# A graph layer on one core: the edge lists' test for order leaves the head, three of four lists go to the edge loop, and the order between stages changes

## The chip, the core and the metric

The kernel runs on one NeuronCore of a Trainium2 chip, as one program from its first load to its last store. The core has four engines that compute, each with an instruction queue of its own that runs in order: TensorE (PE in the profile, its weight loads PEld), VectorE (DVE), ScalarE (ACT) and GpSimd (POOL). A fifth, SyncE (SP), only issues transfers (DMA). Engines wait for each other and for transfers by semaphores. [...]

The metric is the time of one execution on the device in microseconds (us); less is better. Before the change three runs gave a median of 3995.82 us (3989.85 to 4008.74). The profiled execution took 4023.54 us.

## The reference

One layer of a graph network over 6250 nodes with 256 features, 200000 edges that come sorted by their destination, and a second list of 131072 edges in no order. Cut to what matters:

```python
def gat(h, W, a_src, a_dst, src, dst):            # 4 heads of 64
    z = einsum('ni,hid->nhd', h, W)
    es, ed = einsum('nhd,hd->nh', z, a_src), einsum('nhd,hd->nh', z, a_dst)
    e = leaky(es[src] + ed[dst], 0.01)
    ex = exp(e - segment_max(e, dst)[dst])
    alpha = ex / segment_sum(ex, dst)[dst]
    return segment_sum(alpha[:, :, None] * z[src], dst)

def reference(x, src, dst, ...):
    xn = layernorm(x)
    x = x + gat(xn, W, a_src, a_dst, src, dst) + mix(xn, Wqkv, Wout, gamma)
    return x + ffn(layernorm(x), W_gat, ..., W1, b1, W2, b2, edge_index)
```

`mix` is linear attention with 8 heads (softmax of q over features and of k over nodes, then two small matmuls, Wout and a layer norm with `gamma`). `ffn` lets four experts work on each node. How much each counts comes from a second attention over the unordered edges, with 16 features a node, whose sums are normalised with `ln_gamma` and `ln_beta`; the best two experts of a node are mixed.

The input of the first list is sorted, but the kernel has to be right for any list.

## The kernel before

**Tiles.** Nodes are cut into NT = 49 tiles of 128 (the last has 106). Edges are cut into chunks of 128. A chunk's 128 source rows are gathered by one indirect DMA from a table in DRAM, one row for each partition, and summed over destinations by a matmul with a one-hot matrix. For the sorted list every tile gets K1 = 33 chunks, the last 28, so S1 = 1612 chunks in all. Two lists, `src_c` (row to gather) and `dl_c` (which of the tile's 128 nodes), hold what each chunk needs; a copy of the second, `rows_1`, goes to DRAM, to be read back broadcast over the partitions.

**The head** (0 to 138 us) makes the table `ztab` and the lists, side by side:

- `load_x` (L507) loads XB = 7 tiles of x. `project_x` (L520) takes seven tiles at a time: statistics (L527, L528), their rstd chain (L132 to L136, one for the seven), the normalised tile `xn` (L533), two transposes into `ln_tp` (L146), the copy to `xy` (L537), the matmuls into `zp` (L540), the copies into one of eight `zt` buffers (L542 on ACT, L545 on DVE), and the store of the table's rows (L547, on SP's queue).
- Meanwhile `bd` and `bs` (destinations and sources of all edges, 13 blocks of 128 by 128) and `nx` (the destinations moved by one) are loaded on the same queue. `down` (L598) compares `bd` with `nx`: any edge whose destination exceeds the next one's shows an unordered list. The maximum of it (L600) becomes `flag` (L605), which all engines read into a register. Under `tc.If(unordered != 0)` (L610) stands `order_edges`, which sorts the list. Both lists are then stored to DRAM as `d_ord` and `s_ord` (L617), ordered in any case.
- Borders (L629 to L669): the destinations are cast to `fd` (L630), compared with all tile borders (`lt`, L640), counted by matmuls (`cp`, `row`), which gives `start_k`, the edge at which each tile begins. From it, with matmuls into `ip` (L682), comes `at` (L689): where in the ordered list each chunk begins.
- POOL gathers the chunks' edges with 26 indirect DMAs (L697), 13 for each list.
- `lists(b0)` (L705 to L721) is called for b0 = 0, 4, 8 and 12, each call for four blocks of 128 chunks (the last for one). It corrects and masks the local destinations (L708, L712, L713), stores `rows_1` (L714), and transposes both lists through the PSUM tile `e_tp` (L720) into `src_c` and `dl_c` (L721).
- `over` (L742) is set when a tile has more edges than its chunks hold.
- Weights of `mix` are loaded on SP's queue (L753 to L755) behind the table store of tile 41.
- With all of the table stored, the largest source term is found (L198, L190) and the edge loop's gathers begin.

**The edge loop** (138 to 2638 us) takes 202 groups of eight chunks. `FirstEdges` holds a group: gathers (L784), the attention weights, the weighing of gathered rows (`weigh`, L848), the one-hot matrices (`one_hot`, L813), and the matmuls into the tile's sums `ag` (L857). The body for one group, with the parts of the next group between its own, is

```python
            now.weigh(0, 4)
            nxt.terms()
            now.add(sums, g * G1, 0, 4)
            now.weigh(4, 8)
            nxt.one_hot()
            now.add(sums, g * G1, 4, 8)
            groups[g + 2].one_hot_t()
            nxt.terms_sum()
            nxt.sources()
```

with steps of `mix` and sorting steps for the second edge list in the gaps. A finished tile is divided by its weights' sum (L766 to L768), added up (L866), normalised (`n_st` L158, `n_mv` L159, L168), multiplied by `W_gat`, and stored in the second table (`htab` and `htab_0`, L181 and L182).

**Branch and second stage** (2638 to 4022 us). Under `tc.If(many != 0)` (L1116), with `many` read from `over`, stands a slow general path that redoes the first attention for lists which do not fit. With the inputs here it is skipped. The second stage takes the unordered edges in 98 groups (`SecondEdges`, gathers L1321), with the experts' matmuls (L1427, L1447) between. In its group 2 the rows `ln_gamma` and `ln_beta` are loaded and multiplied by a quarter (L1778), and a mask `first_of` is set (L1779 to L1781).

**What sets the order.** A scheduler orders each engine's instructions when the kernel is built, from what each one depends on; the order in the source is not binding. `tc.issue_after(i)` keeps what stands under it behind instruction i. DMA transfers started by SP pass through SP's queue in order, as do the indirect ones through POOL's.

Of the kernel before, what the change touches and what calls it, by code (L numbers as in the profile page):

```python
# [9 lines left out]
F32 = mybir.dt.float32  # L10
# [10 lines left out]
P = 128  # L21
# [43 lines left out]
def gps_layer(ctx: ExitStack, tc: tile.TileContext, a: dict, out: bass.AP):  # L65
# [83 lines left out]
    def second_norm(work, ps, ts_):  # L149
# [15 lines left out]
        for i, t in enumerate(ts_):  # L165
# [15 lines left out]
            SP.dma_start(htab_0[n0 : n0 + n, :], h_all[:n, t, 0:HF])  # L181
            SP.dma_start(htab[n0 : n0 + n, 0:HW], h_all[:n, t, 0:HW])  # L182
# [80 lines left out]
    rows_1 = dram.tile([BS * P * P, 1], BF16, name="rows_1")  # L263

    def order_edges(w, bs, bd):
# [81 lines left out]
        V.tensor_copy(bd, both[:, :, :, 1])  # L347

# [150 lines left out]
    with tc.tile_pool(name="a_x", bufs=1) as ax, tc.tile_pool(name="a_w", bufs=3) as aw, tc.tile_pool(  # L499
# [69 lines left out]
        with tc.tile_pool(name="e_w", bufs=1) as w:  # L569
            bs = w.tile([P, B1, P], I32, name="bs")  # L570
# [3 lines left out]
            G.memset(bs[:, last:], 0)  # L574
            G.memset(bd[:, last:], NT * P)
            G.memset(nx[:, (E1 - 1) // (P * P) :], int(FAR))
            load_blocks(bd, a["dst"], E1)
            load_blocks(nx, a["dst"][1:E1], E1 - 1)
            load_x(XB)
            load_blocks(bs, a["src"], E1)  # L580
# [15 lines left out]

            down = w.tile([P, B1, P], BF16, name="down")
            V.tensor_tensor(down, bd, nx, op=OP.is_gt)  # L598
            d1 = w.tile([P, 1], F32, name="d1")
            V.tensor_reduce(d1, down.rearrange("p b j -> p (b j)"), AX.X, OP.max)  # L600
            flag = w.tile([1, 1], I32, name="flag")
            with tc.tile_pool(name="fl_p", bufs=1, space=PSUM) as ps:
                d2 = ps.tile([1, 1], F32, name="d2")
                T.matmul(d2, d1, ones[:, 0:1], start=True, stop=True)
                V.tensor_scalar(flag, d2, 1.0, None, op0=OP.min)  # L605
            project_x(XB)
            unordered = nc.values_load(
                flag[0:1, 0:1], min_val=0, max_val=1, skip_runtime_bounds_check_because="a count of 0s and 1s, at most 1"
            )
            with tc.If(unordered != 0):  # L610
                with tc.tile_pool(name="ord_w", bufs=1) as ow:
                    order_edges(ow, bs, bd)

            load_x(3 * XB)
            project_x(2 * XB)
            for ord_, b_ in ((d_ord, bd), (s_ord, bs)):
                SP.dma_start(ord_.rearrange("(b r j) o -> r b (j o)", r=P, j=P), b_)  # L617
            with tc.tile_pool(name="e_l", bufs=1) as w, tc.tile_pool(name="e_p", bufs=1, space=PSUM) as ps:
                NX = NT - 1
                room = kx.rearrange("p t d -> p (t d)")  # L620
                used = 0

                def take(a_, b_, dt):
                    nonlocal used
                    used += a_ * b_
# [1235 lines left out]
```

## Time and profile before

| | |
|---|---|
| median of three runs | 3995.82 us (3989.85 to 4008.74) |
| profiled execution | 4023.54 us, its span 4021.7 us |
| mean granted clock of TensorE | 0.784 |
| head | 0 to 138 us |
| edge loop, 202 groups | 138 to 2638 us |
| second stage, 98 groups | 2638 to 4022 us |
| first and last list gather (POOL, L697) | start at 63.79, the last one ends near 96 us |
| first table gather (POOL, L784) | 138.12 us |
| last table gather of the loop (L784) | 2613.98 us |
| first gather of the second table (L1321) | 2642.17 us |

The profile's page gives busy times for the whole span; a stage has to be cut out by its limits in time. In a row of the time line the columns are start, duration, engine, line and operation, tiles written and read with their shapes, how many instructions the row joins, and in brackets how long the engine had been idle before it and what ended that. A suffix q (DVEq, PEq) means the engine's instruction sequencer rather than its arithmetic. "remote" and "issue" stand for a release that the profile does not trace to an instruction.

The page's slices show the span in 40 equal parts, each digit the busy share in tenths:

```profile
PE   5666677755564555546555555446666767677766
DVE  5566666677774776766677566625555546565657
POOL 2466666665665666656666566655556556555552
PEclk8778798877776777777777777767888788888878
```

### The profile page before, as it was taken

Reading aid. Unit: us, or ns where it says so; the run is one execution under the profiler, and the core shown is the slowest. Engines: PE = TensorE matmul, PEld = TensorE weight load, DVE = VectorE, ACT = ScalarE, POOL = GpSimd, SP = SyncE. Lnnn points to the kernel's source line nnn. Section 1 sums busy time; section 2 is a strip of 40 time slices with the busy share of each in tenths; the row PEclk is TensorE's granted clock in tenths of the full one; section 3 lists DMA queues with packets and bytes.
Section 4 is the critical chain, followed back from the end, with each engine's and each line's share of the span. In section 5 each row is a group of like instructions: output and inputs, shape, how many; then the busy total and the mean of one; then the engine's idle time right before and its main releaser. Section 6 shows DMA issues by size and latency. Waiting matters only on the chain. (4 is left out here: it accounts for less than half of the span.)

```text
span 4021.7 us, 36890 instructions
## 1 busy us (share of the span) xinstructions
PE 2498.4 (62%) x10919; PEld 1773.3 (44%) x10920; DVE 2464.6 (61%) x6571; ACT 506.5 (13%) x1319; POOL 2328.2 (58%) x2436
## 2 busy tenths in 40 slices
PE   5666677755564555546555555446666767677766
PEld 4444565544443444434444433324444444444444
DVE  5566666677774776766677566625555546565657
ACT  2200011111110110111111111121111011111112
POOL 2466666665665666656666566655556556555552
PEclk8778798877776777777777777767888788888878
DMA  5443344444443443444444444332222123222221
GB/s 166 131 114 109 108 116 110 119 119 116 122 130 97 116 123 108 120 112 115 133 116 127 113 125 109 104 81 51 45 60 50 42 49 81 53 61 57 59 56 32
DMA packets 248565, 388.33 MB, mean 97 GB/s; under 512 B 73447, under 2 KB 156279, under 8 KB 248090
## 3 DMA queue, kind: packets, MB, share of 16 engines
q0 software_dynamic: 103296, 230.96, 23.1%
q1 hardware_dynamic: 142893, 154.04, 12.6%
q8 instruction: 91, 1.49, 0.1%
q14 instruction: 129, 1.05, 0.1%
q10 hardware_dynamic: 2156, 0.80, 0.1%
HBM read 345.44 MB, written 40.15 MB: 96 GB/s over the span
## 5 line engine op out<-in xcount | busy, mean ns | idle before, releaser
L784 POOL DMA_INDIRECT gt<-ztab,src_c x1612 | 1551.5, 962 | 967.3 <-issue 406.3
L857 PE MATMUL ag<-gt,oh 128*128 128x260 f32 x3224 | 1017.2, 474 | 342.6 <-DVE gt L848 232.0
L1321 POOL DMA_INDIRECT gt<-htab,src x784 | 748.6, 955 | 595.3 <-DVE dv L1390 261.2
L857 PEld LDWEIGHTS ag<-gt,oh 128*128 128x128 f32 x3224 | 754.0, 241 | 527.2 <-DVE gt L848 255.0
L1427 PE MATMUL hp<-xy,w 128*128 128x512 f32 (+1 forms) x832 | 444.3, 657 | 187.2 <-ACT hT L1432 140.5
L1447 PE MATMUL yo<-w,hT 128*128 128x256 f32 x1568 | 446.4, 425 | 111.4 <-issue 63.8
L848 DVE TENSOR_TENSOR gt<-gt,dv 128x1040 f32<-128x1040 f32 x403 | 489.0, 1224 | 13.7 <-issue 12.6
L1447 PEld LDWEIGHTS yo<-w,hT 128*128 128x128 f32 x1568 | 316.5, 209 | 246.2 <-issue 137.2
L883 PE MATMUL m<-wqkv,xy 128*128 128x256 f32 (+1 forms) x784 | 254.6, 464 | 169.5 <-DVE kmax L894 85.3
L1427 PEld LDWEIGHTS hp<-xy,w 128*128 128x128 f32 x832 | 169.0, 216 | 328.5 <-issue 167.3
L883 PEld LDWEIGHTS m<-wqkv,xy 128*128 128x128 f32 (+1 forms) x784 | 171.8, 231 | 217.2 <-DVE kmax L894 91.3
L813 DVE TENSOR_TENSOR oh<-dv,dl_c 128x1024 f32<-128x1024 f32 x202 | 244.0, 1208 | 7.8 <-PE ag L857 5.2
L1432 ACT ACTIVATE hT<-hp,b 128x512 f32<-128x512 f32 (+1 forms) x208 | 133.5, 660 | 479.4 <-remote 172.9
L1371 DVE TENSOR_TENSOR e_sel<-ed,ohq 128x384 f32<-128x384 f32 x98 | 54.1, 552 | 182.4 <-remote 136.8
L213 ACT ACTIVATE src_f<-src_d,shift_c 128x32 f32<-128x32 f32 x202 | 64.9, 321 | 772.5 <-DVE src_d L798 441.4
L381 DVE MAX8 src<-dl 128x8 f32<-128x1024 f32 x128 | 155.5, 1215 | 0.0
L383 DVE MATCH_REPLACE8 dl<-src,dl 128x1024 f32<-128x1024 f32 x127 | 153.5, 1209 | 0.0
L976 PE MATMUL m<-m_sb,qT 128*128 128x256 f32 (+1 forms) x196 | 74.4, 516 | 125.4 <-ACT qT L973 86.8
L1412 DVE TENSOR_REDUCE ag<-ag 128x40 f32<-128x120 f32 x98 | 27.2, 277 | 193.5 <-remote 154.5
L828 PE MATMUL ed<-pw,ohT 128*128 128x24 bf16 x1612 | 71.8, 176 | 106.7 <-DVE ohT L822 46.3
L828 PEld LDWEIGHTS <-ohT 128*128 128x128 bf16 x1612 | 67.1, 100 | 141.6 <-DVE ohT L822 53.6
L836 DVE TENSOR_REDUCE pw<-ed 128x64 f32<-128x192 f32 x202 | 69.6, 344 | 94.9 <-remote 74.6
(374 smaller groups left out, 2745.7 us busy)
## 6 DMA issues: line engine op xcount, KB each, us to landing
br<-rows SPq DMA_DIRECT2D x299, 256.0 KB
gt<-ztab,src_c POOLq DMA_INDIRECT x1612
gt<-htab,src POOLq DMA_INDIRECT x784
early<-ys SPq DMA_DIRECT2D x24, 512.0 KB
ys<-early SPq DMA_DIRECT2D x24, 512.0 KB
ztab<-zt SPq DMA_DIRECT2D x48, 132.0 KB
row<-in_x_dram SPq DMA_DIRECT2D x48, 128.0 KB
out_dram<-ys SPq DMA_DIRECT2D x47, 128.0 KB
```

The costliest lines, as they stand in the source:

```text
L381: V.max(out=srtf[:, 8 * i : 8 * i + 8], in_=keyf)
L383: V.match_replace(out=keyf, in_to_replace=srtf[:, 8 * i : 8 * i + 8], in_values=keyf, imm_value=0.0)
L784: G.indirect_dma_start(out=self.gt[-1][:, c % GH, :], out_offset=None, in_=ztab[:, :], in_offset=bass.IndirectOffsetOnAxis(ap=self.idx[:, ...
L813: V.tensor_tensor(self.oh[:, :n], self.dv[:, None, :P].to_broadcast([P, n, P]), self.dl[:, :, None].to_broadcast([P, n, P]), op=OP.is_equal,)
L828: T.matmul(self.ed[:, c, :], self.ohT[:, c * P : (c + 1) * P], pw3[:, ds(self.tiles[c], 1), :].rearrange("p a b -> p (a b)"), start=True, ...
L848: V.tensor_mul(gz, gz, self.wp[:, c0:c1].unsqueeze(3).to_broadcast([P, c1 - c0, 4, 65]))
L857: T.matmul(sums[t], self.oh[:, c], self.gt[c // GH][:, c % GH, 0:ZW], start=(s0 + c == 0 or chunk_tile[s0 + c - 1] != t), stop=last,)
L883: T.matmul(out_, xy[:, t, j, :n], wqkv[:, j, c0 : c0 + D], start=(j == 0), stop=(j == 1))
L1321: G.indirect_dma_start(out=self.gt[:, c, : tab.shape[1]], out_offset=None, in_=tab[:, :], in_offset=bass.IndirectOffsetOnAxis(ap=self.idx[ ...
L1427: T.matmul(hp[:, :m], wts[e][0][:, c, j * P : (j + 1) * P], xy[:, t0 : t0 + nt, c] if m == nt * P else xy[:, t0, c, :m], start=(c == 0), s ...
L1432: S.activation(h[:, :m], hp[:, :m], AF.Gelu, bias=b1[:, e, j : j + 1])
L1447: T.matmul(yo[:n], hT[j][:, o : o + n], wts[e][1][:, j, :], start=(j == 0 and e < EARLY), stop=(j == 3))
```

## The change

The change has seven parts.

1. `d_ord` and `s_ord` are filled by DRAM-to-DRAM copies of the input (`copy_list`, and stores of constant `pads` for the end), behind the table store of tile 6. `bs` and its load go. The load of `nx` moves behind the copies. The register read and the branch at L610 go. `down` and its maximum stand later (behind `xn` of tile 20), and the result is joined with the count of edges that sets `over`. So an unordered list now takes the slow path under `many`, which begins with `order_edges`, the stores and a second call for the borders.
2. The border computation is a function, `borders`, and `base` lies in borrowed room.
3. Only `lists(ps, 0)` stands in the head. The other three calls stand in the edge loop, at the end of groups 2, 6 and 10, and `e_tp` has one buffer.
4. The weights of `mix` are loaded behind the table store of tile 21 in place of tile 41.
5. Of a tile's two `htab` stores the second is kept behind the first.
6. In the last four groups of the edge loop the next group's `one_hot`, `terms_sum` and `sources` are kept behind the present group's last weighing.
7. In group 2 of the second stage the scaling of the two rows and the setting of `first_of` are kept behind that group's one-hot.

The diff, with the moved text of `borders` left out:

```diff
@@ second_norm
-            SP.dma_start(htab_0[n0 : n0 + n, :], h_all[:n, t, 0:HF])
-            SP.dma_start(htab[n0 : n0 + n, 0:HW], h_all[:n, t, 0:HW])
+            with tc.issue_after(SP.dma_start(htab_0[n0 : n0 + n, :], h_all[:n, t, 0:HF]).ins):
+                SP.dma_start(htab[n0 : n0 + n, 0:HW], h_all[:n, t, 0:HW])
@@ new functions
+    def copy_list(to, flat):
+        n = E1 // P
+        SP.dma_start(to[0 : P * n, :].rearrange("(p c) o -> p (c o)", p=P), flat[0 : P * n].rearrange("(p c) -> p c", p=P))
+        if E1 % P:
+            SP.dma_start(to[P * n : E1, :].rearrange("(p c) o -> p (c o)", p=1), flat[P * n : E1].rearrange("(p c) -> p c", p=1))
+    def borders(w, ps, take, bd):
+        fd = take(B1, P, F32)
+        V.tensor_copy(fd, bd)
...
+        return row
@@ head
-            bs = w.tile([P, B1, P], I32, name="bs")
...
             load_blocks(bd, a["dst"], E1)
-            load_blocks(nx, a["dst"][1:E1], E1 - 1)
             load_x(XB)
-            load_blocks(bs, a["src"], E1)
             load_x(2 * XB)
...
-            down = w.tile([P, B1, P], BF16, name="down")
-            V.tensor_tensor(down, bd, nx, op=OP.is_gt)
-            d1 = w.tile([P, 1], F32, name="d1")
-            V.tensor_reduce(d1, down.rearrange("p b j -> p (b j)"), AX.X, OP.max)
...
+            with tc.issue_after(zst[XB - 1].ins):
+                for to, flat, i in ((d_ord, a["dst"], 1), (s_ord, a["src"], 0)):
+                    copy_list(to, flat)
+                    SP.dma_start(to[E1:, :].rearrange("(p c) o -> p (c o)", p=pp), pads[:, i])
+                load_blocks(nx, a["dst"][1:E1], E1 - 1)
             project_x(XB)
-            unordered = nc.values_load(
-                flag[0:1, 0:1], min_val=0, max_val=1, skip_runtime_bounds_check_because="a count of 0s and 1s, at most 1"
-            )
-            with tc.If(unordered != 0):
-                with tc.tile_pool(name="ord_w", bufs=1) as ow:
-                    order_edges(ow, bs, bd)
-
             load_x(3 * XB)
             project_x(2 * XB)
-            for ord_, b_ in ((d_ord, bd), (s_ord, bs)):
-                SP.dma_start(ord_.rearrange("(b r j) o -> r b (j o)", r=P, j=P), b_)
...
+                row = borders(w, ps, take, bd)
...
+                        tp = ps.tile([P, 4, P], F32, name="e_tp", bufs=1)
...
+                with tc.issue_after(xnv[3 * XB - 1].ins):
+                    down = w.tile([P, B1, P], BF16, name="down")
+                    V.tensor_tensor(down, bd, nx, op=OP.is_gt)
+                    d1 = w.tile([P, 1], F32, name="d1")
+                    V.tensor_reduce(d1, down.rearrange("p b j -> p (b j)"), AX.X, OP.max)
+                d2 = w.tile([1, 1], F32, name="d2")
+                d2p = aps.tile([P, 264], F32, name="zp")
+                T.matmul(d2p[:1, 0:1], d1, ones[:, 0:1], start=True, stop=True)
+                V.tensor_copy(d2, d2p[:1, 0:1])
...
-                for b0, t in zip(range(0, BS, 4), (NT - 17, NT - 10, NT - 3, NT - 2)):
-                    with tc.issue_after(zmm[t].ins), tc.issue_after(xnv[t].ins), tc.issue_after(zst[t].ins):
-                        lists(b0)
+                with tc.issue_after(zmm[NT - 17].ins), tc.issue_after(xnv[NT - 17].ins), tc.issue_after(zst[NT - 17].ins):
+                    lists(ps, 0)
...
+                V.scalar_tensor_tensor(most, d2, FAR, most, op0=OP.mult, op1=OP.max)
                 V.tensor_scalar(over, most, float(K1 * P), None, op0=OP.is_gt)
...
-    with tc.issue_after(zst[NT - 8].ins):
+    with tc.issue_after(zst[3 * XB].ins):
         SP.dma_start(wqkv, a["L0_mix_Wqkv"].rearrange("(j p) f -> p j f", p=P))
@@ edge loop
+            behind = lambda: tc.issue_after(now.weighed.ins) if g >= NGR - 4 else nullcontext()
             if nxt:
-                nxt.one_hot()
+                with behind():
+                    nxt.one_hot()
             mix_hops()
             now.add(sums, g * G1, 4, 8)
...
             if nxt:
-                nxt.terms_sum()
-                nxt.sources()
+                with behind():
+                    nxt.terms_sum()
+                    nxt.sources()
...
+            if g % 4 == 2 and g // 4 + 1 < (BS + 3) // 4:
+                lists(ps, 4 * (g // 4 + 1))
@@ under many
+            with tc.tile_pool(name="ord_w", bufs=1) as ow:
+                bs = ow.tile([P, B1, P], I32, name="bs")
...
+                order_edges(ow, bs, bd)
+                for ord_, b_ in ((d_ord, bd), (s_ord, bs)):
+                    SP.dma_start(ord_.rearrange("(b r j) o -> r b (j o)", r=P, j=P), b_)
+                with tc.tile_pool(name="bo_p", bufs=1, space=PSUM) as ps_:
+                    borders(ow, ps_, Room().take, bd)
@@ second stage
+                    with tc.issue_after(groups[g].oh_i.ins):
+                        for quarter in (lg, lb):
+                            V.tensor_scalar(quarter, quarter, 0.25, None, op0=OP.mult)
+                        V.memset(first_of, 0.0)
...
```

## The prediction, made before the changed kernel had run

> **What bounds the kernel now.** I read the page's busy shares first, then the costliest groups, then the time line at the three places that the change touches: the head (0 to 138 us), the start of the edge loop, and the passage from the first stage to the second (2605 to 2643). All times are of one profiled execution: span 4021.7 us plus 1.8 around it, 4023.5.
>
> ```profile
> PE 2498.4 (62%) x10919; PEld 1773.3 (44%) x10920; DVE 2464.6 (61%) x6571; ACT 506.5 (13%) x1319; POOL 2328.2 (58%) x2436
> PE 13%; another core or an unknown queue 11%; DVE 6%; issue 3%; ACT 0%; DMA 0%; POOL 0%; DVEq 0%; ACTq 0%; POOLq 0%
> L784 POOL DMA_INDIRECT gt<-ztab,src_c x1612 | 1551.5, 962 | 967.3 <-issue 406.3
> ```
>
> No engine is over 62%, and the printed chain covers about a third of the span, so neither settles the matter. The third line does for the loop: 1612 gathers take 1551.5 us, and with 0.30 us between two of them 1.25 us each, so 8 chunks need 10.0 us of POOL. The loop takes (2638-138)/202 = 12.4 us a group: POOL's pace, plus hand-offs to VectorE and TensorE. Both loops' POOL and PE sequences stay as they are, but for six groups of transposes. So the change acts at the ends of the stages, where shares over 4022 us show nothing.
>
> The head, by stretches (columns: length; busy time of PE, PEld, DVE, ACT, POOL; granted clock; DMA share; GB/s):
>
> ```profile
> 25.00:50.00 25.00, 20.30 (x90) 14.99 (x89) 19.91 (x74) 10.87 (x41) 2.22 (x4) 0.86 0.67 209
> 60.00:75.00 15.00, 12.55 (x58) 10.08 (x58) 4.83 (x29) 3.86 (x15) 8.68 (x9) 0.77 0.42 129
> 75.00:100.00 25.00, 5.10 (x12) 3.23 (x12) 2.90 (x12) 1.73 (x6) 16.07 (x17) 0.52 0.23 65
> 100.00:125.00 25.00, 22.97 (x106) 18.02 (x106) 19.18 (x80) 14.28 (x52) 0.00 (x0) 0.87 0.30 91
> ```
>
> From 25 to 50 PE and DVE are both about 80% busy: each matters. From 75 to 100 the head stands nearly still, with DMA at 0.23; that is while POOL issues its 26 list gathers (63.79 to 96.2 us). From 100 on PE is 92% busy, 1.5 us a tile: the tail of the head belongs to PE.
>
> **The branch.**
>
> ```profile
> 29.41 0.74 DVE L533 TENSOR_SCALAR xn<-xa,mv,ln_r 128x256 f32<-128x256 f32 x2
> 33.08 2.30 DVE L533 TENSOR_SCALAR xn<-xa,mv,ln_r 128x256 f32<-128x256 f32 x3 [2.94 <-DVEq L610]
> ```
>
> The bracket is idle time and its releaser: DVE stood 2.94 us at L610, the test for unordered edges. [...] The row has one, so I take 2.9, between 1 (PE's own wait there was 0.97) and 4.
>
> **Work moved to the front.** In the changed kernel's queues the border work (cast of the destinations 0.99 us, comparison 1.20, sum 0.80, the two rank computations 1.03 and 1.88) stands on DVE before the first batch's rstd chain; in this trace it runs from 39 to 48. That is 5.9 us, so the first transpose on PE, at 17.24 now, comes near 23. DVE is even in the sum. PE is not: it is busy 37.4 us of 17.24 to 60, so 5.4 of the 6 us of late start exceed its slack unless idle time later falls away. The branch's stall and the bunched border work at 39 to 48, where PE waits for DVE, make up most of that. Cost between 0 and 6; I take 2. `down` and its maximum (1.88 + 1.88) move from 19 to just before `at`: even in the sum.
>
> **List copies.** d_ord and s_ord are now written from DRAM to DRAM, six transfers on SP's queue ahead of the second batch's table stores, and the load of `bs` goes. [...] The trace has the old stores at 33.01 and 37.74 and their first reader at 63.79: 26 us of cover. [...] The `nx` load stands behind the copies; its reader, `down`, is 20 us later.
>
> **The lists.** Each list of four blocks costs DVE 0.69 + 0.42 + 0.42 for preparation and twice 0.69 for the casts, and PE eight transposes of 0.273 us. The preparation of all four stays in the head (the queues show it); transposes and casts of the lists at 4, 8 and 12 go to the loop: 18 transposes, 4.9 us of PE, and 3.3 us of DVE. Only what stands ahead of the last tile's matmuls was on PE's path: 8 of the 18 transposes, 2.2 us, and part of the 1.7 us that PE waited for their one buffer. Gain 1 to 5; I take 3.
>
> **The head's tail.**
>
> ```profile
> 131.77 0.25 SPq L547 DMA_DIRECT2D ztab<-zt  x1
> 136.81 0.50 DVE L198 TENSOR_REDUCE f_m<-src 128x4 f32<-128x196 f32 x1 [2.31 <-DMA ztab<-zt]
> 138.12 0.95 POOL L784 DMA_INDIRECT gt<-ztab,src_c  x1 [41.95 <-DVE f_col L190]
> ```
>
> The last table store takes about 5 us to land, which f_m waits for, and the first gather follows 1.3 us later. Between 123 and 132 the mix weights share the queue with these stores; they now go out some 17 tiles sooner. I take 1.5 of the 5 (0 to 3). The casts that ran at 132 to 135 leave, but the landing hid them: 0.
>
> **The stall.** If it comes as it did, the head gains 2.9 - 2 + 0 + 3 + 1.5 = 5.4. If it shrinks, DVE's preparation of the third list, which needs the 24th gather, is what waits instead: gathers begin at about 59 at best, end 26 x 1.25 = 32.5 later, land by 95; about 24 us of DVE work and the 6 us of tail follow: first gather at 122 to 125, a gain of 13 to 16. I take a little of that, 9 in all, with 0 to 16 as ends. SP has a new order too: four list stores and a load of `row` that waits for all gathers stand between the stores of tiles 30 to 36. They wait for the same gathers; inside these ends.
>
> **The loop.** Six transpose groups and casts now stand in its first 12 groups. There DVE is 75% busy in steady state (151.31 of 200 us, 1000 to 1200), so a 0.69 us cast fits; I take 1 us of cost (0 to 8.2, their whole PE and DVE time).
>
> **The passage.** Columns as in the time line above:
>
> ```profile
> 2628.52 0.16 DVE L766 TENSOR_SCALAR rd<-ag 128x4 f32<-128x4 f32 x1 [5.42 <-PE ag L857]
> ...
> 2629.84 0.43 DVE L158 BATCH_NORM_STATS2 n_st<-kx 106x6 f32<-106x256 f32 x1
> 2631.95 0.17 DVE L1778 TENSOR_SCALAR L_ffn_ln_gamma<-L_ffn_ln_gamma 128x16 f32<-128x16 f32 x1 [1.68 <-DMA L_ffn_ln_gamma<-in_L_ffn_ln_gamma_dram]
> 2632.44 0.17 DVE L1778 TENSOR_SCALAR L_ffn_ln_beta<-L_ffn_ln_beta 128x16 f32<-128x16 f32 x1 [0.31 <-DMA L_ffn_ln_beta<-in_L_ffn_ln_beta_dram]
> 2632.53 0.18 DVE L159 BATCH_NORM_AGGREGATE n_mv<-n_st 106x2 f32<-106x6 f32 x1
> ```
>
> In the last tile's chain, with all waiting for it, DVE stops for two weight rows of the next stage. Statistics end at 2630.27 and their aggregate starts at 2632.53; without the scalings it starts at about 2630.3: gain 2.2 (2.0 to 2.6 with the small memsets). The scalings then cost 0.3 us behind the second stage's one-hot of group 2, beside gathers.
>
> In the last four groups, weighing goes ahead of the next one-hot. At 2608.52 a one-hot (1.22) stood before the weighing at 2610.97, for which PE waited until 2612.25; POOL in turn waited 4.43 us for PE's `ag` before 2605.22. Bringing a weighing forward by one one-hot each time is worth 1.2, by two 2.4. The delayed one-hot may delay the next group's sum by as much. I take 2 (-1 to 4). The swap of the two table stores: 0.3 us of issue, taken as 0.
>
> **Sum.** 9 - 1 + 2.2 + 2 = 12.2 off 4023.5: 4011.3. The profiled execution stands 27.7 above the median of 3995.8 (0.7%), so I carry the difference to the median: 3983.6, **3983**. Shown runs of before lie 19 us apart, so less than 0.5% (20 us, 3975.8 to 4015.8) can't be told from no change; the sum is inside that.
>
> **Rivals.** *Shrunken stall, 3973.* The head gains 16, the passage 2.6 + 4, the loop pays 0: 22.6 off, 3973. For it: the head has the slack, with DMA idle. Against: nothing in the change touches the 26 gathers' rate. 0.27.
>
> *Gain swallowed, 3996.* The late first transpose costs its full 6 us and the lists gain 1: head 0; the swap and the loop cancel the passage's 2.2. For it: PE's load up to 60. 0.17.
>
> *Slower, 4025.* One mechanism: the moved transposes use one PSUM buffer, so each of six groups waits on PE for DVE's cast of the one before, in PE's in-order queue ahead of the loop's matmuls. And in this stretch hand-offs from PE are slow:
>
> ```profile
> 167.16 0.36 DVE L836 TENSOR_REDUCE pw<-ed 128x64 f32<-128x192 f32 x1 [11.53 <-remote]
> 176.28 0.42 DVE L894 TENSOR_TENSOR kmax<-kmax,m 128x256 f32<-128x256 f32 x1 [8.58 <-remote]
> ```
>
> DVE waited 11.53 and 8.58 us for results of PE whose work was over. Six hand-offs at some 7 us are 42; with the other gains of 13, 29 slower: 4025. It decides from (20 + 13)/6 = 5.5 us per hand-off. Against: in the head the same hand-off took 0.4 to 0.75 us, and four of the six stand later than this stretch. 0.18.
>
> That the change doesn't do what it says: the queues keep the lists' preparation in the head, which is counted.
>
> **How the numbers follow.** Forecast 0.38 (its own range 3972 to 3996), shrunken stall 0.27, swallowed 0.17, slower 0.18. Faster by over 0.5% are four fifths of the shrunken-stall case and a fifth of the forecast: 0.29. Slower: the last case and a few hundredths of the swallowed: 0.20. Within: 0.51. From 3956 (17 us below the shrunken case, nearly the 19 by which the runs of before differ) to 4016 lie about 8 in 10.
>
> **What would show it.** Right: no idle time at L610's place; first transpose near 23 us; first gather of the table near 129; the aggregate of the last tile right behind its statistics; `ag` in the last groups 1 to 2 us sooner; the same 12.4 us a group. Wrong: the first table gather at 138 or later; a new wait named `e_tp` on PE or DVE from 130 to 280 us; SP's table stores held behind the load of `row`; or a loop whose length moves by over 10 us, which no step above accounts for.

## The result, and the profile after

The changed kernel is slower: median 4005.72 us (3991.83 to 4035.41, 20 runs) beside 3995.36 (3959.3 to 4024.12, 20 runs) for the kernel before on the same chip. The ratio, taken run against run by rounds, is 1.0044 with a 95% interval of 1.0025 to 1.0063, so 10 to 25 us. On a second chip of this speed it was 1.0013 (0.9986 to 1.0040), which by itself can't be told from no change. The forecast was 3983.

The profiled execution took 4020.26 us. Its page beside the lines shown of before: busy times, chain, table gathers, then the slices. Lines of the kernel have moved (L784 is now L796, L848 is L860).

```profile
PE 2476.4 (62%) x10919; PEld 1761.7 (44%) x10920; DVE 2466.3 (61%) x6572; ACT 504.4 (13%) x1319; POOL 2330.7 (58%) x2437
...
PE   5564677755564565556555545547767677777775
...
DVE  5565566676776675775667666625555555656556
...
POOL 2465666666666566666666656645556555555551
PEclk8777888877777777777777777667888888888887
...
PE 15%; another core or an unknown queue 9%; issue 4%; DVE 4%; ACT 0%; POOL 0%; DMA 0%; DVEq 0%; ACTq 0%; SPq 0%; POOLq 0%
...
L796 POOL DMA_INDIRECT gt<-ztab,src_c x1612 | 1555.4, 965 | 969.9 <-issue 406.9
```

Nothing here tells the kernels apart: the sums over 4018 us hide everything. The stages do it, divided at the first table gather, the last table gather, and the first gather of the second table. Each number is a difference of such starts in one trace:

| us | head | loop | passage | second stage |
|---|---|---|---|---|
| before | 138.1 | 2475.9 | 28.2 | 1379.5 |
| before, second chip | 139.4 | 2465.6 | 27.1 | 1371.9 |
| after | 135.3 | 2479.9 | 31.4 | 1371.9 |
| after, second chip | 135.3 | 2476.9 | 31.1 | 1374.3 |

By the means the head gained 3.5 us, the loop lost 7.7 and the passage lost 3.6; with 2.6 less in the second stage, which nothing in the change explains, the spans are 5.2 us longer. Single executions of one kernel lie up to 65 us apart, so four profiles give the places and signs; they do not add up to the 10 to 25 us.

**The head.** Stretches of after; columns as in the prediction's table:

```profile
25.00:50.00 25.00, 24.79 (x124) 19.12 (x123) 18.99 (x91) 12.61 (x49) 0.00 (x0) 1.00 0.69 200
60.00:75.00 15.00, 6.87 (x31) 4.67 (x29) 5.49 (x26) 3.53 (x13) 11.34 (x13) 0.84 0.74 212
75.00:100.00 25.00, 9.54 (x24) 6.38 (x24) 4.43 (x18) 3.31 (x13) 12.21 (x13) 0.57 0.29 80
100.00:125.00 25.00, 21.69 (x110) 16.88 (x108) 18.65 (x82) 14.71 (x56) 0.00 (x0) 1.00 0.48 145
```

From 25 to 50 PE is now 99% busy (24.79 of 25): the branch's stall and the wait on border work are gone. But the still stretch begins sooner. From 60 to 75 PE falls from 12.55 to 6.87. The gathers start at 58.5 instead of 63.8, and the still stretch came forward by about as much. The time line of after at the end of the head:

```profile
129.97 0.17 ACT L609 COPY src<-zp 106x8 f32<-106x8 f32 x1 [0.23 <-DVE zt L608]
134.61 0.50 DVE L198 TENSOR_REDUCE f_m<-src 128x4 f32<-128x196 f32 x1 [4.68 <-DMA ztab<-zt]
...
135.25 0.95 POOL L796 DMA_INDIRECT gt<-ztab,src_c  x1 [44.38 <-DVE f_m L198]
```

The last table store is issued at 130.0, and `f_m` (L198) can start 4.6 us later; in before it took 5.0. So the earlier weights (part 4) brought the landing little nearer. The first gather then follows `f_m` by 0.6 us in place of 1.3.

**The passage.** All engines of after, in one time line:

```profile
2619.17 0.40 DVE L168 TENSOR_SCALAR row<-kx,n_mv,n_r 128x256 f32<-128x256 f32 x1
2619.48 0.25 DVE L810 TENSOR_TENSOR src_d<-gt,most 128x16 f32<-128x16 f32 x2
2620.18 0.63 PE L172 MATMUL m<-ident,row 128*128 128x128 f32 x2
...
2620.85 0.37 ACT L173 COPY xy<-m 128x256 f32<-128x256 f32 x1 [5.92 <-PE m L172]
2621.24 1.28 ACT L213 ACT_TABLE_LOAD   x1
2622.53 0.32 ACT L213 ACTIVATE src_f<-src_d,shift_c 128x32 f32<-128x32 f32 x1
...
2623.80 0.17 DVE L179 COPY h_all<-m 128x16 f32<-128x16 f32 x1 [4.07 <-PE m L177]
...
2623.96 0.21 DVE L852 TENSOR_TENSOR pw<-pw,src_f 128x64 f32<-128x64 f32 x1
...
2624.45 2.38 DVE L860 TENSOR_TENSOR gt<-gt,dv 128x1040 f32<-128x1040 f32 x2
...
2634.26 0.43 DVE L158 BATCH_NORM_STATS2 n_st<-kx 106x6 f32<-106x256 f32 x1
2634.72 0.18 DVE L159 BATCH_NORM_AGGREGATE n_mv<-n_st 106x2 f32<-106x6 f32 x1
```

The aggregate now follows its statistics at once, as part 7 intends. Part 6 does not do what it was meant to. The next group's `src_d` now waits until the present group is weighed (2616.49 to 2617.71, on DVE). By then the norm of tile 47 has come in between: ScalarE's copy L173 for that tile stands ahead of the exponential of `src_f`, and a table load of 1.28 us between the two. On DVE L179 stands ahead of L852 and waits for PE 4.07 us. So the weighing (L860) comes 9.3 us after the last table gather (2615.16); in the trace of before it came 4.4 after it (2618.38, gather at 2613.98). There the table load and the exponential were through before the norm of tile 47 reached TensorE and ScalarE; the trace of before at this place:

```profile
2612.25 3.37 PEld L857 LDWEIGHTS ag<-gt,oh 128*128 128x128 f32 x16 [0.15 <-DVE gt L848]
...
2615.38 1.28 ACT L213 ACT_TABLE_LOAD   x1 [1.29 <-DVE pw L836]
...
2616.67 0.32 ACT L213 ACTIVATE src_f<-src_d,shift_c 128x32 f32<-128x32 f32 x1
...
2617.67 0.18 DVE L798 TENSOR_TENSOR src_d<-gt,most 128x16 f32<-128x16 f32 x1 [0.24 <-DMA gt<-ztab,src_c]
...
2618.38 2.38 DVE L848 TENSOR_TENSOR gt<-gt,dv 128x1040 f32<-128x1040 f32 x2
...
2618.99 0.37 ACT L173 COPY xy<-m 128x256 f32<-128x256 f32 x1 [0.64 <-PE m L172]
```

### The profile page after: what moved, and what is told of

Read it like the earlier page. It is cut to its first block, busy times and chain, and to the rows that moved or that the text cites. A ratio compares the mean times of both kernels' runs of the same rounds, so it can differ in the third digit from the quotient of the medians.

```text
span 4018.5 us, 36813 instructions
## 1 busy us (share of the span) xinstructions
PE 2476.4 (62%) x10919; PEld 1761.7 (44%) x10920; DVE 2466.3 (61%) x6572; ACT 504.4 (13%) x1319; POOL 2330.7 (58%) x2437
## 5 line engine op out<-in xcount | busy, mean ns | idle before, releaser
L796 POOL DMA_INDIRECT gt<-ztab,src_c x1612 | 1555.4, 965 | 969.9 <-issue 406.9
L869 PE MATMUL ag<-gt,oh 128*128 128x260 f32 x3224 | 1006.3, 470 | 329.1 <-DVE gt L860 187.6
L860 DVE TENSOR_TENSOR gt<-gt,dv 128x1040 f32<-128x1040 f32 x403 | 489.0, 1223 | 17.3 <-issue 17.2
L848 DVE TENSOR_REDUCE pw<-ed 128x64 f32<-128x192 f32 x202 | 69.5, 344 | 105.2 <-remote 98.4
```

The costliest lines, as they stand in the source:

```text
L796: G.indirect_dma_start(out=self.gt[-1][:, c % GH, :], out_offset=None, in_=ztab[:, :], in_offset=bass.IndirectOffsetOnAxis(ap=self.idx[:, ...
L860: self.weighed = V.tensor_mul(gz, gz, self.wp[:, c0:c1].unsqueeze(3).to_broadcast([P, c1 - c0, 4, 65]))
L869: T.matmul(sums[t], self.oh[:, c], self.gt[c // GH][:, c % GH, 0:ZW], start=(s0 + c == 0 or chunk_tile[s0 + c - 1] != t), stop=last,)
```

## The experiments

The runs fell on several chips. On two of them the kernel before takes 3995 to 4021 us, on the others about 3208; a kernel is compared only with the kernel before on its own chip. They are called the 4000 us chips and the 3208 us chips below. The commonest instructions of VectorE and GpSimd take the same time on both (L860 1.22 us, a gather 0.95). Over half of the difference of 800 us is in long idle times of PE: those of over 6 us, counted from 150 us on, are 63 with 620 us in the trace of before on a 4000 us chip, 22 with 182 us on a 3208 us chip. On a 3208 us chip the loop runs close to POOL's pace, 40.0 us for 32 gathers at the least and 40.3 in the median; on a 4000 us chip the median is 48.

The theories after the result: part 6 costs in the passage; part 3 costs in the loop; or part 1 costs behind the branch, where the sorting's memory holds back loads. The rival is that the head alone failed to give what it should. (The expectations count the 26 list gathers with the others: their gathers 122 to 186 are the table's 96 to 160, eight groups from group 12 on, and their 1610 to 1626 are the table's 1584 to 1600. Their "fast" and "slow" chips are the 3208 us and the 4000 us chips.)

**First set, on a 3208 us chip (before 3208.3).** Part 6 undone:

```diff
-            behind = lambda: tc.issue_after(now.weighed.ins) if g >= NGR - 4 else nullcontext()
+            behind = lambda: nullcontext()
```

> The changed kernel with the last four groups' order taken back (part 6 undone), all else kept. Passage theory: in the changed kernel the next group's attention terms come behind the weighing and so behind the norm chain of tile 47 and a reload of ScalarE's exp table; undone, the stretch from the last table gather to the first gather of the second table falls from 31.4 us to 27 to 29, and the time by 3 to 4 us (ratio to before about 1.0035). List theory (the moved lists slow the loop): the stretch may move, the time stays at 1.0044 within 0.0005.

Ratio 1.0015 (1.0006 to 1.0023): without part 6 it is slower here. Part 3 undone (all four lists in the head again):

```diff
-                with tc.issue_after(zmm[NT - 17].ins), ...:
-                    lists(ps, 0)
+                for b0, t in zip(range(0, BS, 4), (NT - 17, NT - 10, NT - 3, NT - 2)):
+                    with tc.issue_after(zmm[t].ins), ...:
+                        lists(ps, b0)
...
-            if g % 4 == 2 and g // 4 + 1 < (BS + 3) // 4:
-                lists(ps, 4 * (g // 4 + 1))
```

> The changed kernel with all four list calls back in the head (part 3 undone). List theory: the hand-offs of the one transpose buffer no longer stand in the loop, so gathers 122 to 186 are not 18 us late and the time falls by 8 to 15 us, to a ratio of 0.998 to 1.002. Passage theory: the first table gather comes 2 to 5 us later (137 to 140), the loop is as long within its scatter, and the time stays or grows by up to 5 us (1.004 to 1.006).

Ratio 1.0008 (1.0000 to 1.0017). The branch without the sorting (the block under `ord_w` is left out, so an unordered list is no longer sorted there; the input here doesn't enter it):

```diff
-            with tc.tile_pool(name="ord_w", bufs=1) as ow:
-                bs = ow.tile([P, B1, P], I32, name="bs")
...
```

> The changed kernel without the sorting of the list, its stores and the second call for the borders under the branch between the stages; for sorted lists the result is unchanged. The loads of the second stage's small rows then stand ahead of the branch again, as before the change. Passage theory with the branch as its second part: the stretch from last table gather to first gather of the second table falls by 1.5 to 3 us from 31.4, the first expert matmul comes 2 to 4 us sooner after it, and the time falls by 2 to 5 us. List theory: nothing over 1 us.

Ratio 0.9996 (0.9988 to 1.0004), its passage 20.8 us. The loads that move are visible in after on the 4000 us chip, where two lines from the passage's time line show the load behind the branch, and its first reader:

```profile
2646.21 0.35 SPq L1272 DMA_DIRECT2D b1r<-in_L_ffn_b_dram  x1
...
2648.11 0.28 PE L1290 MATMUL bp<-ident,b1r 16*128 16x16 f32 x1 [2.43 <-DMA b1r<-in_L_ffn_b_dram]
```

By then the second table's gathers run (2646.58), so little waits for it. Yet the traces show a cost at one place. From the last copy of tile 48 (L180) to the first gather of the second table it is 5.9 us in this kernel, and 7.4 to 7.9 us in all eight traces of kernels with both the sorting under the branch and lists in the loop. In the other eleven, which lack one of the two, it is 5.4 to 5.9. So the two together cost about 2 us there; why it takes both was not found. In the times it is inside the intervals. Part 6 in all groups:

```diff
-            behind = lambda: tc.issue_after(now.weighed.ins) if g >= NGR - 4 else nullcontext()
+            behind = lambda: tc.issue_after(now.weighed.ins)
```

> The changed kernel with the order of part 6 in all 202 groups in place of the last four, which multiplies its cost by about 50. If holding the next group's one-hot and terms behind the weighing costs 0.5 to 1 us a group, as the passage theory has it, the loop grows by 100 to 200 us; if it gains 0.5 us a group, as the forecast had it, it shrinks by 100; if the order doesn't matter inside the loop, it moves by less than 20 us.

One execution: 3210.5 beside a median of 3208.3. Neither a loss nor a gain for each group shows: on this chip, where POOL's gathers set the pace, the order inside a group did not matter.

**Second set, on a 4000 us chip (before 4020.69).** After and before again, the head's parts 1 and 2 alone (parts 3 to 7 undone), and part 6 alone on top of before. The edits of the last two, the first against after (one of its five places is shown), the second against before:

```diff
-    with tc.issue_after(zst[3 * XB].ins):
+    with tc.issue_after(zst[NT - 8].ins):
         SP.dma_start(wqkv, a["L0_mix_Wqkv"].rearrange("(j p) f -> p j f", p=P))
...
```

```diff
+            behind = lambda: tc.issue_after(now.weighed.ins) if g >= NGR - 4 else nullcontext()
             if nxt:
-                nxt.one_hot()
+                with behind():
+                    nxt.one_hot()
...
```

> The changed kernel as it is, timed again beside the kernel before on one chip. If the slowdown belongs to the change and not to the chip of the first comparison: 1.001 to 1.004. Passage theory: its stretch from last table gather to first gather of the second table is longer than the kernel before's on the same chip. List theory: its loop is longer than the kernel before's by over 8 us. Both theories: first table gather 3 to 8 us sooner than before.

> The kernel before, for a profile on the same chip as the other runs of this call. Expected by both theories: ratio 1.000; head 3 to 8 us longer than the changed kernel's; its small loads of the second stage ahead of the branch.

> Parts 1 and 2 alone: no branch in the head, copied lists, sorting under the later branch; lists, weights, loop, last groups and second stage as before. Passage theory: the branch's side effect alone makes it slower than before by 2 to 4 us in the passage, and the head gains 3 us or less, so 0.999 to 1.001. List theory: without the moved lists the loop is as before, so it is faster, 0.998 to 0.9995.

> The kernel before with part 6 alone (last four groups). By the first four runs, where undoing it left a passage of 28 us against 22: it shortens the passage by 4 to 6 us, ratio 0.998 to 0.9990. By my first reading of the trace of after (terms held behind the norm chain of tile 47): it lengthens it by 2 to 4 us, 1.0005 to 1.001.

Measured: after 1.0013 (0.9986 to 1.0040); before in one execution 4006.05 us; parts 1 and 2 alone 0.9993 (0.9963 to 1.0023); part 6 alone **1.0028 (1.0002 to 1.0053)**, slower by 1 to 21 us. The passage sorts these traces without exception: 31.4, 31.1 and 31.3 with part 6 (after, after again, part 6 alone), 28.2, 27.1 and 25.7 without (before, before again, parts 1 and 2). Part 6 alone has the same wait at the same place, here in ScalarE's time line:

```profile
2632.67 1.28 ACT L213 ACT_TABLE_LOAD   x1
2633.97 0.32 ACT L213 ACTIVATE src_f<-src_d,shift_c 128x32 f32<-128x32 f32 x1
```

and in VectorE's:

```profile
2635.24 0.17 DVE L179 COPY h_all<-m 128x16 f32<-128x16 f32 x1 [4.07 <-PE m L177]
```

Here nothing else of the change is in the kernel, so in the passage the cause is shown. Its size is that of the passage, 4 us; the rest of the 11 us by which part 6 alone is slower in the middle of its interval was not found in the traces.

The passage can be divided further. In the table, "sum ready" is the time from the last table gather to the first step on the last tile's sum (L766, in after L778); "statistics to aggregate" is L158 to L159 of that tile, and "to second table" runs from its last copy (L180) to the first gather of the second table:

| us, 4000 us chips | sum ready | statistics to aggregate | to second table |
|---|---|---|---|
| before, two traces | 14.5, 13.3 | 2.7, 2.7 | 5.5, 5.6 |
| parts 1 and 2 alone | 14.1 | 0.5 | 5.6 |
| part 6 alone | 18.0 | 0.5 | 5.9 |
| after, two traces | 17.8, 17.6 | 0.5, 0.5 | 7.7, 7.5 |

By the means of before and after, part 6's place lost 3.8 us, the scalings gave 2.2 back, and the stretch behind the branch lost 2.1: together the 3.6. The second column also falls where part 7 is absent. With parts 1 and 2 alone the two rows are loaded behind the branch (at 2647.04), so their scaling can't stand in the tile's chain. The kernel without the sorting (on a 3208 us chip), where they load ahead of it again, keeps the short distance of 0.5 us by part 7. Either edit is enough. With part 6 alone the scalings merely fall behind the aggregate (2647.81).

Of the head, parts 1 and 2 alone gave 1.8 us on this chip (137.6 beside 139.4), with part 3 it is 4.1 (135.3).

**Third set, on a 3208 us chip (before 3208.3).** After, both parts undone one by one again, and both at once:

> The changed kernel once more, as the measure for the three others on this chip. On a chip of about 4000 us: stretch from table gather 122 to 186 (groups 12 to 20) 104 to 110 us, gathers 1610 to 1626 31 us, passage 31 us, ratio 1.001 to 1.005. On a chip of about 3200 us: loop at 10.0 us a group throughout, passage 21 to 23 us, ratio 1.000 to 1.001.

> Part 3 undone (lists in the head), on the chip of after_third. List theory, on a slow chip: gathers 122 to 186 take 91 to 97 us as in all kernels that keep the lists in the head, the head is 2 to 5 us longer, and the time falls by 7 to 12 us against after_third. If the long stretch comes from something else in the change it stays over 104. On a fast chip: head 4 us longer, loop as it is, time 1 to 4 us more than after_third.

> Part 6 undone, on the chip of after_third. Passage theory, slow chip: gathers 1610 to 1626 fall from 31 to 23 us and the passage from 31 to 26 to 28, and the time by 8 to 12 us. Fast chip: passage 28 against 22 and the time 5 us more, as in the first call.

> Parts 3 and 6 undone together. If the two are the cause and add up, on a slow chip the time falls by 15 to 20 us against after_third and comes 5 to 8 us below the kernel before (0.998 to 0.9985), with gathers 122 to 186 at 91 to 97 us, 1610 to 1626 at 23, passage 26 to 28. On a fast chip: 5 to 9 us more than after_third.

After 0.9998 (0.9990 to 1.0006): no loss on this chip. Part 3 undone 1.0000 (0.9992 to 1.0008), part 6 undone 1.0018 (1.0011 to 1.0024), both 1.0016 (1.0009 to 1.0022). So part 6 *gains* here: the passage is 21.9 us in after and 27.8 to 28.4 in the three traces with it alone undone. Why the sign turns is seen in two time lines. First VectorE with part 6 undone, on the 3208 us chip:

```profile
2164.37 0.18 DVE L810 TENSOR_TENSOR src_d<-gt,most 128x16 f32<-128x16 f32 x1 [3.27 <-DMA gt<-ztab,src_c]
...
2165.09 2.38 DVE L860 TENSOR_TENSOR gt<-gt,dv 128x1040 f32<-128x1040 f32 x2
```

`src_d` of the last group waits 3.27 us for the last gather to land, in DVE's in-order queue ahead of a weighing that needs nothing of it. Then after on the 3208 us chip:

```profile
2158.04 0.17 DVE L179 COPY h_all<-m 128x16 f32<-128x16 f32 x1 [0.64 <-PE m L177]
...
2159.24 0.23 DVE L852 TENSOR_TENSOR pw<-pw,src_f 128x64 f32<-128x64 f32 x1 [0.96 <-ACT src_f L214]
...
2159.74 2.38 DVE L860 TENSOR_TENSOR gt<-gt,dv 128x1040 f32<-128x1040 f32 x2
```

Part 6 has put the weighing ahead of that landing: it starts 0.4 us after the last gather is issued (2159.38), and the waits for tile 47 are 0.64 and 0.96 us. On a 3208 us chip POOL is last into the passage, so compute waits for gathers. On a 4000 us chip POOL itself had waited 4.04 us for PE at 2606.37, so the gathers have landed before compute gets there (`src_d` waited 0.24 us in before), and part 6 has no wait to remove.

**Fourth set, meant for a 4000 us chip, but run on a 3208 us chip (before 3208.06).** Before's stages, parts 3 and 6 undone, and parts 1 and 2 alone:

> The kernel before, for its stages' times. Slow chip: head 138 to 139.5, gathers 122 to 186 94 to 98 us, 1610 to 1626 23, passage 27 to 28. Fast chip: head 121 to 126, loop 2036 to 2042, and, if the loss of the other parts lies in the passage (sorting under the branch), a passage of 20 to 23 us without part 6; if it lies in the loop or the second stage, one of these is 5 us shorter than 2040 or 1023.

> Part 3 undone. Slow chip, list theory: gathers 122 to 186 back to 91 to 98 us, the other two stretches as in the changed kernel (31 and 31). If stalls only sit elsewhere by accident: any of the three may move. Fast chip: as in the two calls before, ratio 1.000 to 1.001.

> Part 6 undone. Slow chip, passage theory: passage 26 to 28.5 us and gathers 1610 to 1626 back to 23; 122 to 186 stays at 104 to 110. If the order gains here as on the fast chips, the passage grows to 35 or more. Fast chip: 1.0015 to 1.0018 with a passage of 28.

> Parts 1 and 2 alone. Slow chip: as in its first run, head 137 to 138, passage 25 to 27, 0.997 to 1.002. Fast chip: if the sorting moved under the branch is what costs the fast chips 6 us, 1.001 to 1.002 with a passage 3 to 6 us longer than before's; if the early weights or the last small reorderings cost it, 0.9990 to 1.0000.

Before in one execution 3209.54 us. Part 3 undone 1.0007 (0.9999 to 1.0015), part 6 undone 1.0017 (1.0010 to 1.0025), parts 1 and 2 alone 1.0024 (1.0013 to 1.0035). Stages on 3208 us chips:

| us | head | loop | passage |
|---|---|---|---|
| before | 117.1 | 2038.1 | 28.2 |
| parts 1 and 2 alone | 123.4 | 2044.8 | 26.6 |
| part 3 undone (three traces) | 123.0 to 123.3 | 2037.6 to 2041.2 | 21.0 to 22.0 |
| after | 118.0 | 2041.4 | 21.9 |

Parts 1 and 2 *lengthen* the head by 6.3 us, although they start the list gathers 7.9 us sooner (57.7 and 65.6). The stretch from 75 to 100 us, first before, then parts 1 and 2 alone:

```profile
75.00:100.00 25.00, 21.18 (x110) 16.82 (x110) 19.46 (x79) 13.37 (x50) 18.46 (x19) 1.00 0.54 152
```

```profile
75.00:100.00 25.00, 10.01 (x40) 7.73 (x39) 7.88 (x37) 4.56 (x18) 11.61 (x13) 0.66 0.31 87
```

PE's work halves. The time line of parts 1 and 2 alone names the wait:

```profile
91.88 0.06 DVE L932 MEMSET vt<- 128x2 f32 x1 [15.03 <-DMA kx<-s_ord,at]
...
93.18 3.45 PE L603 MATMUL zp<-src,xy 128*128 128x264 f32 x7 [14.65 <-DVE zt L608]
```

The memset of `vt`, a tile of `mix` that nobody needs before the loop, waits for the landing of the lists' gathers (the last was issued at 89.32), though it reads nothing of them, and in DVE's queue it stands ahead of the tiles. The 15.03 us come back as 14.65 us of PE. In before the list work stood where the gathers had already landed; its longest such wait was 1.70 us. With part 3 a list's preparation (L709) still waits 8.12 us for such a landing, and PE 7.62 us; the head goes from 123 to 118 (122.5 in the kernel with part 6 in all groups, which the traces do not explain).

**Fifth set, on a 3208 us chip (before 3209.55).** If that is the cause, the waits moved behind the tiles must give the head what the earlier gathers promise. The first kernel:

```diff
-                with tc.issue_after(zmm[NT - 17].ins), ...:
+                with tc.issue_after(zmm[NT - 9].ins), ...:
                     lists(ps, 0)
-            V.memset(vt[:, :, P : P + 1], 1.0)
+            with tc.issue_after(xnv[NT - 1].ins):
+                V.memset(vt[:, :, P : P + 1], 1.0)
-                SP.dma_start(xt[:n], a["x"][n0 : n0 + n, :])
+                with tc.issue_after(zst[NT - 1].ins):
+                    SP.dma_start(xt[:n], a["x"][n0 : n0 + n, :])
-                lists(ps, 4 * (g // 4 + 1))
+                with tc.issue_after(xnv[NT - 1].ins):
+                    lists(ps, 4 * (g // 4 + 1))
```

The second has the same edits to `vt` and the row load, but all lists in the head, behind tiles NT - 11, NT - 7, NT - 3 and NT - 2.

> The changed kernel with the first list call behind tile 40, the preparation of the other three behind the last tile's normalisation, and the first loads of the mixing step's input rows behind the last table store, so that nothing in the head's queues stands before a gather that has not landed. Head theory (the in-order waits for the gathers cost what the earlier gathers gained): fast chip: first table gather at 107 to 113 us in place of 118, no idle time over 3 us on VectorE between 60 and 100, ratio 0.996 to 0.998. If the late first tiles are what costs the head, it stays at 116 to 119 and the ratio at 1.000. Slow chip: gathers 122 to 186 still 104 to 110 us, head 130 or less if the stall shrinks.

> The same with all four lists in the head (part 3 undone), called behind tiles 38, 42, 46 and 47. Head theory, fast chip: first table gather at 111 to 117 us in place of 123, ratio 0.998 to 0.9995. If the late first tiles cost the head: 121 to 124. Slow chip, list theory: gathers 122 to 186 take 91 to 98 us, against 104 to 110 of x1 on the same chip.

Ratios **0.9960 (0.9946 to 0.9973)** and **0.9953 (0.9939 to 0.9966)**: 3198.63 and 3195.77 us, faster than before and, by after's 0.9998 on another chip of this speed, than after. The head is 107.1 and 107.7 us. The first kernel's stretch:

```profile
75.00:100.00 25.00, 22.31 (x111) 17.68 (x112) 16.74 (x71) 14.49 (x55) 11.51 (x12) 1.00 0.64 200
```

PE is back at 22.31. The two share the moves of `vt` and the row load, and the first list behind later tiles; which of these is worth how much was not separated. Nor was either run on a 4000 us chip.

## Why the prediction was wrong

The forecast was a gain of 12 us that can't be told from no change; measured was a loss of 10 to 25. In the profiles of the 4000 us chips three terms of the sum missed: the passage (4.2 gained by the forecast, 3.6 lost), the head (9 gained, 3.5 gained) and the loop (1 lost, 7.7 lost). For the passage the runs show the cause. For the other two it stays open on these chips, and the three together do not make up the whole 10 to 25.

**Last groups, "I take 2 (-1 to 4)": wrong in sign on the 4000 us chips, and the step that failed.** The gain was read from a wait that was hardly there: a one-hot stood before the weighing at 2610.97, "for which PE waited until 2612.25". The row of before at 2612.25 has an idle time of 0.15 us, as PE had other matmuls until then. And the cost counted only the one-hot: "The delayed one-hot may delay the next group's sum by as much." Part 6 holds back `terms_sum` and `sources` as well, and these start a chain DVE, ScalarE, DVE, whose exponential then falls behind tile 47's norm and a table load. Measured: the last tile's sum is ready 3.8 us later behind the last table gather, with the wait of 4.07 us at L179 in after and in part 6 alone. Part 6 alone is slower by 0.02 to 0.53%. Where gathers are late (3208 us chips) the same edit gains 6, more than the range's 4, for it removes a wait of 3.27 us that the trace of before on a 4000 us chip did not have (0.24).

**Scalings, -2.2: right in size.** 2634.26 and 2634.72, back to back. That part 7 did it is not shown, since parts 1 and 2 alone do the same. Against it stand 2.1 us behind the branch, which no term had.

**Head in all, -9: measured -3.5 on 4000 us chips, +1 on 3208 us ones.** The branch's stall went and the first transposes came at 22.64 us, as predicted ("near 23"); the 2.9 taken for the stall is the idle time in the row at L610 (2.94 us), and what its end alone was worth was not measured apart. The late first transposes cost nothing. The prediction has it that "5.4 of the 6 us of late start exceed its slack", but the 5.4 us is the slack itself, PE's idle time, which can take the late start up. It did: in the first 60 us PE ran 183 matmuls in after and 169 in before. The 0 in the head's sum is for the list copies; no run shows their cost apart. In after they are issued from 36.76 to 39.99 us, two of the six with 0.2 KB each, and the first gather that reads the lists starts at 58.49, behind 42.72 us of POOL's idle time that ended with VectorE's `at` (L690), not with a copy. These gathers start 5 to 8 us sooner than before, as the shrunken-stall step assumed.

On 3208 us chips what failed is "DVE's preparation of the third list, which needs the 24th gather, is what waits instead", which was priced as if tiles could go on beside it. In these traces a waiting instruction on an in-order queue stops the tiles behind it; parts 1 and 2 alone showed 15.03 us of that, and moving those waits gave the head 10 us against before. The shrunken stall's 13 to 16 were thus nearly there to be had, by an edit that the change did not contain.

On 4000 us chips the head's shortfall **stays open**. PE falls off from 60 to 75 (12.55, now 6.87), but VectorE's longest idle times from 60 to 125 us (8.51 us in after, 8.09 in before) are put down to "issue", not to a gather, and the list preparation at 90.60 in after starts without a wait. PE's longest there, 10.65 us, is for a copy of ScalarE. Nor do the gathers by themselves make the still stretch from 75 to 100 that the prediction saw: before on a 3208 us chip issues the same gathers there and keeps PE busy for 21.18 of the 25 us. Neither kernel of the fifth set ran on such a chip.

**The head's tail, -1.5: measured about -0.4.** The landing takes 4.6 us where it took 5.0. Another 0.7 came behind it, from `f_m` to the first gather, which no term had.

**Lists, -3:** about 5 us on 3208 us chips (123 to 118), and at most 2.3 on the second 4000 us chip (137.6 to 135.3, with part 4), both in the range of 1 to 5.

**Loop, +1 (0 to 8.2): +7.7 by the means, and only partly explained.** Both traces of after on 4000 us chips are 11 to 18 us longer than the four without moved lists over eight groups from group 12 on (109.5 and 108.1 us, against 91.4 to 97.1). In that stretch of after stands the slower rival's mechanism once (VectorE's and TensorE's rows of one time line):

```profile
315.27 0.29 DVE L722 CAST dl_c<-e_tp 128x128 bf16<-128x128 f32 x1 [12.23 <-remote]
...
316.08 1.22 PE L895 MATMUL m<-wqkv,xy 128*128 128x256 f32 x2 [13.61 <-DVE kmax L906]
```

The last list's cast waited 12.23 us for transposes that PE had done at 302.4; in the second trace of after the same cast waited 11.61 us. But the loss does not stand in the loop's total: from table gather 192 to 1584 after is 15 us shorter than before by the means. What then equals the 7.7 is one wait of POOL, of 10.0 us, at about 2580 in both traces of after. Table gathers 1584 to 1600 take 31.1 us in both, and 22.6 to 23.3 in the four others, part 6 alone among them, so it is not part 6 alone that makes it. On the 3208 us chips, with the same code, part 3 undone changes the loop by less than 4 us. The run that would decide, part 3 undone on a 4000 us chip, was meant for the fourth set and fell on the other kind. So the cause of both waits **stays open**, and with it the cause of such hand-offs of PE at all.

**The rivals.** Slower, 4025, named a real kind of wait, but six hand-offs at 7 us were not there: one of about 12 is, in each trace. Gain swallowed, 3996, had the size nearer, for the wrong reason: the late transpose cost nothing. Shrunken stall, 3973, did not come: from 60 to 100 us PE worked 17.7 us in before and 16.4 in after. No case had the passage as a whole lose.

## What to carry to other kernels

Before an edit starts a transfer sooner, find out which in-order queue waits for its landing and what stands behind that wait (here list gathers that started 7.9 us sooner made the head 6.3 us longer, with one wait of 15.03 us): list the readers, put each behind the work that doesn't need them, down to a memset that reads nothing of it. An edit that holds a group of instructions behind another must be priced by the whole chain it starts, over every engine, and by who enters the gap. Here such an order paid only where the thing it waits past was late; check which side is late at that very place, since the same edit gained 6 us where gathers were last and lost 4 where compute was. And a wait is read from the row's idle time, not from the order in which two rows stand.

## What the runs showed of the hardware that was not expected

- Chips differ: the same kernel takes 3208 us on some and 3995 to 4021 on others. Granted TensorE clock is 0.855 and 0.784 in the mean, the commonest instructions of DVE and POOL take equally long (1.22 and 0.95 us), and idle times of PE of over 6 us are 22 (182 us) and 63 (620 us). What causes them the traces do not show. The kind of chip turns the sign of an edit: part 6 undone is 1.0018 where part 6 alone is 1.0028.
- Code which did not run here moved transfers: with the sorting under the branch the loads of the second stage's small rows stand behind it (in after `b1r` is issued at 2646.21 and read at 2648.11), without it ahead of it (in before issued at 2628.51, read at 2640.4). That the reason is the memory it is given is the author's guess, not shown.
